# An earlier rank for the work that feeds TensorE, in a four-layer attention kernel on one core

## The chip, the core and the metric

The kernel runs on one core of a Trainium2 chip. A core has TensorE (matrix products, written to PSUM), VectorE, ScalarE, GpSimd and the DMA queues, the busiest of which is issued by SyncE (SP). The profile calls them PE (with PEld for weight loads), DVE, ACT, POOL and SP. The metric is the device time of one execution in microseconds: lower is better. All data are 32-bit floats.

## The reference

The input x has 16 samples of 256 channels by 32 x 32 positions (1024 tokens). Four layers follow each other.

```python
# layer 0: group norm, self-attention over 1024 tokens of width 256, projection, residual
xn = group_norm(x, gamma, beta)
q, k, v = jnp.split(jnp.einsum('bchw,oc->bohw', xn, w_qkv) + b_qkv[None, :, None, None], 3, axis=1)
attn = jax.nn.softmax(jnp.einsum('bnc,bcm->bnm', q, k) / math.sqrt(C), axis=-1)
out = jnp.einsum('bnm,bmc->bnc', attn, v)
x = jnp.einsum('bchw,oc->bohw', out, w_proj) + b_proj[None, :, None, None] + residual
# layer 1: a gate of one value per position
weight3 = jax.nn.relu(_conv3x3(jnp.concatenate([mean_c(x), max_c(x)], axis=1), w1, b1))
x = x * jax.nn.sigmoid(_conv3x3(mean_c(x) + max_c(x) + weight3, w2, b2))
# layer 2: as layer 0 with its own weights
# layer 3: q and k of width 32, logits clipped to [-10, 10], softmax, v of width 256
energy = jnp.clip(jnp.einsum('bqn,bqm->bnm', q, k) * scale, -10.0, 10.0)
x = gamma[0] * jnp.einsum('bcm,bnm->bcn', v, jax.nn.softmax(energy, axis=-1)) + x
```

Here `mean_c` and `max_c` stand for the mean and the maximum over channels.

## The kernel before

**Tiling.** Tokens are tiled in 8 tiles of 128, channels in 2 chunks of 128. Query-key weights and value-projection weights are multiplied together once at the start (`fold`, `fold3`), so that an attention has one product for t, one for the logits, one for the values and one for the weighted sum. The larger products are made with seven block products in place of eight. This needs combinations of blocks: sums and differences of the left blocks (`combine`, L902 to L905), of t (`logits`, L642 to L645), of the values (`value_sums`, L557 to L561) and of the exponentials (`weighted`, L698, L699, L746, L751), made by VectorE. A block of the result is the sum of several products in different PSUM banks. In `seven`, ScalarE copies one bank out (`copy`; L672 in the logits, L925 in the values, L947 for t) and VectorE adds the other bank to it (`plus`, L603). `weighted` has the same with L743, L756, L759 and L768 as copies, L725 as sums, and the reciprocals of the row sums at L755 and L762. All matrix products of these helpers are recorded on one line, L571. The eight PSUM banks are one pool.

**The stages of one sample** (`sample`): load; norm of layer 0 (`group_norm`, called by `head`); attention of layer 0 (`attend`: t, values, then for each half of the queries `logits` with exponentials L682 and L684, and `weighted`, which adds the normalised result to the residual at L732); planes for the gate (L992, L1000); the gate (`gate_of`) and its scaling (L1018, L1022); a turn from token order to channel order by VectorE transposes (L519) and a DMA through memory on the SP queue (`send`); norm of layer 2; attention of layer 2; another turn and send; layer 3 (`clipped_attend`: q and k at L1072 with their bias at L1084 and L1088, values, logits at L1107 with exponentials L1123 and clip L1128, `weighted`); strip transposes (L494), bias (L487) and the store. `attend` and `weighted` serve layers 0 and 2; `weighted` serves layer 3, too.

**The order of the work.** The program text is written as Python generators. Two lanes, one for even and one for odd samples, take turns: each `yield` hands over to the other lane, and lane 1 starts 30 steps (`OFFSET`) behind lane 0. Constants W_* put empty steps into a lane at places with a long latency, such as the gate and the sends; `chores` are small pieces of work handed out one a step. The order in which instructions are written gives each its rank. The framework's planner then goes through the program with its own estimates of durations: whenever an engine comes free, it issues, of the instructions for that engine whose inputs are ready, the one of the lowest rank. What comes out is a fixed order for each engine, and each engine keeps to it on the chip, waiting on semaphores for its inputs. `keep_in_program_order` holds an instruction behind all that is written before it on its engine.

An alternative path for inputs outside of the fast path's range (`general_path`) is in the program, but doesn't run here.

## Time and profile before

| what | value |
|---|---|
| time, median of 3 runs | 2700.45 us (2700.41 to 2702.32) |
| span of the profiled execution | 2702.3 us |
| the profiled execution's own time | 2702.32 us, the slowest of the three |
| instructions | 47717 |
| mean granted TensorE clock | 0.997 of full |
| bytes read from memory, written | 69.58 MB, 50.33 MB |
| matmuls, VectorE and ScalarE instructions | 18998, 4242, 2810 |

The page of the profile gives each engine's busy time and its share of the span; a table by stretches gives the same within a stretch, with the number of instructions in brackets, then the granted clock, the busy share of the DMA engines and GB/s. A line of waits reads "who waited <- for whom: us in total, times, longest us". A line in order of time reads "start, us, engine, line, operation, what it writes <- what it reads, partitions x elements, count", and in square brackets the idle time of the engine before it and what ended it.

### The profile page before, as it was taken

The page shows a single profiled execution, that of the slowest core. Times are in us where ns is not written, and L with a number is a line of the kernel's source. Part 1 is how long each engine was busy: PE and PEld are TensorE (multiplying, and loading weights), DVE is VectorE, ACT ScalarE, POOL GpSimd, SP SyncE. Part 2 cuts the span into 40 slices and gives each one's busy share as a digit, 9 for nine tenths or more (in the row PEclk, how much of TensorE's full clock was granted, in tenths as well). Part 3 has the DMA queues.
Part 4 walks back from the last instruction along what each step waited for, and adds up shares of the span by engine and source line. Part 5 has one row for each costly group of instructions (what it writes and reads, how often), then busy time and mean ns, then how long its engine had stood idle before and what let it go on. Part 6 is the DMA issues. An engine that isn't in the chain of part 4 may idle for free.

```text
span 2702.3 us, 47717 instructions
## 1 busy us (share of the span) xinstructions
PE 2658.2 (98%) x18998; PEld 2366.0 (88%) x18998; DVE 2153.9 (80%) x4242; ACT 1327.9 (49%) x2810; POOL 45.4 (2%) x118
## 2 busy tenths in 40 slices
PE   8999999999999999999999999999999999999997
PEld 6888988888988889889889898988989889898897
DVE  7988886888778887788867888678887788868776
ACT  3454455544455445544455544554454544545443
POOL 1000000000000000000000000000000000000000
PEclk9999999999999999999999999999999999999999
DMA  4021111212111120211201212112111121101111
GB/s 115 1 63 48 56 32 24 63 48 63 25 46 50 42 76 9 55 48 48 63 16 48 63 35 61 32 32 63 48 48 32 32 63 55 40 17 34 52 34 41
DMA packets 134823, 123.07 MB, mean 46 GB/s; under 512 B 10689, under 2 KB 125633, under 8 KB 134593
## 3 DMA queue, kind: packets, MB, share of 16 engines
q1 hardware_dynamic: 132720, 118.63, 15.7%
q8 instruction: 152, 2.49, 0.4%
q10 hardware_dynamic: 1872, 1.31, 0.2%
q14 instruction: 79, 0.64, 0.1%
HBM read 69.58 MB, written 50.33 MB: 44 GB/s over the span
## 4 chain that ended last, share of the span: by engine, by line
PE 81%; DVE 13%; ACT 4%; issue 2%; DMA 1%; POOL 0%; DVEq 0%; SPq 0%; ACTq 0%
PE b_l L571 15%; PE c_l L571 11%; PE af_l L571 11%; PE sb_l L571 10%; PE sc_l L571 8%; PE sf_l L571 4%; PE sa_l L571 3%; PE vb_l L571 3%; PE tb_l L571 3%; PE vc_l L571 2%; PE tc_l L571 2%; PE s L1107 2%; DVE e_l L603 1%; DVE vt L603 1%; PE vf_l L571 1%
## 5 line engine op out<-in xcount | busy, mean ns | idle before, releaser
L672 ACT COPY e_l<-sb_l 128x512 f32<-128x512 f32 x384 | 222.5, 584 | 217.9 <-PE sb_l L571 216.7
L571 PE MATMUL sb_l<-t_l,x 128*128 128x256 f32 x1024 | 262.0, 386 | 0.3
L571 PE MATMUL b_l<-vt,e_l 128*128 128x128 f32 x2048 | 251.8, 275 | 0.0
L571 PEld LDWEIGHTS b_l<-vt,e_l 128*128 128x128 f32 x2048 | 244.2, 192 | 5.4 <-issue 2.3
L571 PEld LDWEIGHTS sb_l<-t_l,x 128*128 128x128 f32 x1024 | 180.5, 191 | 40.1 <-ACT e_l L672 11.2
L682 ACT ACTIVATE e_l<-e_l 128x512 f32<-128x512 f32 x256 | 160.9, 630 | 86.6 <-DVE e_l L603 85.7
L684 ACT ACTIVATE e_l<-e_l 128x1024 f32<-128x1024 f32 x128 | 135.5, 1059 | 118.4 <-DVE e_l L603 118.4
L571 PE MATMUL c_l<-tv,cb_l 128*128 128x129 f32 x1536 | 189.0, 275 | 0.2 <-DVE cb_l L698 0.2
L571 PEld LDWEIGHTS c_l<-tv,cb_l 128*128 128x128 f32 x1536 | 180.3, 191 | 6.9 <-PE qk L1072 3.1
L603 DVE TENSOR_TENSOR e_l<-sc_l,e_l 128x512 f32<-128x512 f32 x128 | 88.0, 687 | 116.6 <-PE sc_l L571 114.9
L925 ACT COPY vt<-vb_l 128x512 f32<-128x512 f32 x144 | 84.5, 587 | 147.2 <-PE vb_l L571 146.1
L487 ACT ACTIVATE xr<-xr,bstrip 128x128 f32<-128x128 f32 (+1 forms) x376 | 134.4, 443 | 44.1 <-DVE xr L494 44.1
L1123 ACT ACTIVATE e<-s 128x512 f32<-128x512 f32 x256 | 131.8, 606 | 22.1 <-PE s L1107 21.4
L756 ACT COPY acc_l<-c_l 128x256 f32<-128x256 f32 x96 | 35.4, 368 | 212.3 <-DVE ri_l L755 151.8
L571 PE MATMUL sc_l<-tc_l,xs_l 128*128 128x256 f32 x512 | 134.0, 384 | 2.3 <-DVE vt L603 2.3
L571 PE MATMUL af_l<-tv,e_l 128*128 128x128 f32 x1024 | 131.6, 278 | 4.3 <-ACT e_l L682 4.3
L571 PE MATMUL sc_l<-t_l,xs_l 128*128 128x256 f32 x512 | 133.0, 382 | 0.8
L571 PE MATMUL sa_l<-t_l,x 128*128 128x256 f32 x512 | 132.4, 381 | 0.0
L571 PE MATMUL sf_l<-tc_l,x 128*128 128x256 f32 x512 | 131.7, 380 | 0.0
L571 PE MATMUL sb_l<-tc_l,xs_l 128*128 128x256 f32 x512 | 131.7, 379 | 0.0
L571 PEld LDWEIGHTS af_l<-tv,e_l 128*128 128x128 f32 x1024 | 121.3, 192 | 10.8 <-ACT e_l L682 7.7
L1128 DVE TENSOR_SCALAR e<-e 128x1024 f32<-128x1024 f32 x128 | 83.0, 687 | 59.0 <-ACT e L1123 59.0
(245 smaller groups left out, 5984.6 us busy)
## 6 DMA issues: line engine op xcount, KB each, us to landing
x<-mid_x SPq DMA_DIRECT2D x64, 512.0 KB, 3.3
xr<-in_x_dram SPq DMA_DIRECT2D x64, 256.0 KB, 4.9
mid_x<-t_z SPq DMA_DIRECT2D x128, 128.0 KB, 2.3
mid_x<-t_l SPq DMA_DIRECT2D x128, 128.0 KB, 2.3
x<-in_x_dram SPq DMA_DIRECT2D x62, 256.0 KB, 4.0
out_dram<-xr SPq DMA_DIRECT2D x124, 128.0 KB, 2.3
raw_l<-in_w_l_dram SPq DMA_DIRECT2D x1, 1024.0 KB, 6.9
raw_l<-in_w_l_dram SPq DMA_DIRECT2D x2, 256.0 KB, 5.5
```

Of the source, the lines that this page charges most:

```text
L487: nc.scalar.activation(y[:, s, ts], y[:, s, ts], AF.Identity, bias=bias[:, s : s + 1])
L571: mm = nc.tensor.matmul(out, left, right, start=fresh and m == 0 and (lone or i == 0), stop=(m == len(pairs) - 1), skip_group_check=True,)
L603: nc.vector.tensor_tensor(dst, src, dst, ALU.add)
L672: nc.scalar.copy(block(i, j), ps.rearrange("p (m n) -> p m n", m=2))
L682: nc.scalar.activation(part, part, AF.Exp)
L684: nc.scalar.activation(e[:, m : m + 2, :], e[:, m : m + 2, :], AF.Exp)
L756: nc.scalar.copy(acc[:, hi, c2], c[:, :, :P])
L925: nc.scalar.copy(block(i, j), ps.rearrange("p (m n) -> p m n", m=TPH))
L1107: nc.tensor.matmul(ss[g][:, j * 2 * P : (j + 1) * 2 * P].rearrange("p (t g j) -> p t g j", t=TPH, g=2), qk[gs, mh, 1 - blk, j * P : (j + 1 ...
L1123: nc.scalar.activation(by_strip[:, :, :, qa], ss[g].rearrange("p (m t n) -> p m t n", m=2, t=TPH), AF.Exp,)
L1128: nc.vector.tensor_scalar(part, part, EXP_MIN, EXP_MAX, ALU.max, ALU.min)
```

## The change

A block `with soon():` is put around instructions of VectorE, ScalarE and (one in each norm) GpSimd. Inside such a block an instruction gets a rank that is 100 lower than its place in the program text; after the block the rank goes on where it was before it. Matrix products, DMAs and everything outside of the blocks keep their rank. The planner is otherwise the same, and so are the instructions and their dependencies.

In the blocks are: all of `group_norm` (the general path passes `ExitStack`, which does nothing), `value_sums`, the sums of `seven`, the combinations, copies and exponentials of `logits`, the combinations, copies, sums and reciprocals of `weighted`, `combine`, and the copies of `values` and of t. Not in them are: the additions L732, planes, gate and scaling, turns, strip transposes and bias, the weight folding, the checks, and of layer 3 the q and k writes (L1084, L1088), the exponentials (L1123) and the clip (L1128).

```diff
+URGENT = 100
...
+    soon = functools.partial(tc.high_priority, offset=URGENT)
...
-def group_norm(nc, k, small, xt, out, gamma, beta, nm, keep=None):
+def group_norm(nc, k, small, xt, out, gamma, beta, nm, soon, keep=None):
...
+    with soon():
+        st = small.tile([P, CC, 2, 6], FP, tag="st", name=f"st_{nm}", bufs=2)
...
     yield
...
+    with soon():
+        rst = small.tile([P, 6], FP, tag="rst", name=f"rst_{nm}", bufs=2)
...
     yield
...
+    with soon():
+        a = small.tile([P, CC], FP, tag="a", name=f"a_{nm}")
...
             t1, t2, t4 = (tv[:, i, :, :P] for i in range(3))
-            nc.vector.tensor_tensor(t1, b[0][1], b[0][0], ALU.subtract)
...
+            with soon():
+                nc.vector.tensor_tensor(t1, b[0][1], b[0][0], ALU.subtract)
...
-                nc.vector.tensor_tensor(dst, src, dst, ALU.add)
+                with soon():
+                    nc.vector.tensor_tensor(dst, src, dst, ALU.add)
...
+            with soon():
+                nc.vector.tensor_tensor(t1, t3, bl(0, 0), ALU.subtract)
...
-                    nc.scalar.copy(block(i, j), ps.rearrange("p (m n) -> p m n", m=2))
+                    with soon():
+                        nc.scalar.copy(block(i, j), ps.rearrange("p (m n) -> p m n", m=2))
...
                     if step >= 2:
+                        with soon():
+                            m = (step - 2) * TPH + 2 * g
...
+            with soon():
+                nc.vector.tensor_tensor(s1, a(1, 0), a(1, 1), ALU.add)
+                nc.vector.tensor_tensor(s3, a(0, 0), s3, ALU.subtract)
...
             def plus(ts, cs, ps):
-                nc.vector.tensor_tensor(acc[:, ts, cs], ps, acc[:, ts, cs], ALU.add)
+                with soon():
+                    nc.vector.tensor_tensor(acc[:, ts, cs], ps, acc[:, ts, cs], ALU.add)
...
             c = bank(f"c_{nm}_{h}")[:, : 2 * (P + 1)].rearrange("p (i c) -> p i c", i=2)
             go(s1, t1, c, lone=False)
+            with soon():
+                nc.vector.reciprocal(ri[:, n1 : n1 + 2], c[:, :, P])
+                nc.scalar.copy(acc[:, hi, c2], c[:, :, :P])
             yield
...
+            with soon():
+                nc.vector.tensor_tensor(left("s1"), left("21"), left("22"), ALU.add)
...
             def copy(i, j, ps):
-                nc.scalar.copy(block(i, j), ps.rearrange("p (m n) -> p m n", m=TPH))
+                with soon():
+                    nc.scalar.copy(block(i, j), ps.rearrange("p (m n) -> p m n", m=TPH))
...
             def t_copy(i, j, ps):
+                with soon():
+                    nc.scalar.activation(
+                        t_block(i, j),
```

## The prediction

> **What bounds the kernel now.** I read the first part of the page (busy shares), then the same in three stretches, then TensorE's waits, then the order of time at the places where TensorE stood still. Busy shares and stretches:
>
> ```profile
> span 2702.3 us, 47717 instructions
> PE 2658.2 (98%) x18998; PEld 2366.0 (88%) x18998; DVE 2153.9 (80%) x4242; ACT 1327.9 (49%) x2810; POOL 45.4 (2%) x118
> ...
> 0.00:100.00 100.00, 86.36 (x466) 71.03 (x467) 81.03 (x244) 42.02 (x81) 12.01 (x38) 0.97 0.31 78
> 100.00:2600.00 2500.00, 2485.08 (x17790) 2214.18 (x17788) 2004.31 (x3880) 1248.69 (x2643) 32.75 (x77) 1.00 0.16 45
> 2600.00:2702.00 102.00, 86.73 (x747) 80.74 (x745) 68.57 (x120) 37.20 (x87) 0.60 (x3) 0.96 0.12 33
> ```
>
> In each stretch the first figure after its length is TensorE's busy time. TensorE is the bound: idle 13.6 us in the first 100, 15.3 us in the last 102 and only 14.9 us in the 2500 between. That understates its stalls, because a matmul's record is longer than its place in the stream: 16 matmuls of 128 columns fill 1.95 us with records of 275 ns each, so they start every (1950 - 275) / 15 = 112 ns, and a stall of up to 275 - 112 = 163 ns shows no idle time. I therefore took the starts themselves from the trace. Between 100 and 2600 us, starts that came more than 60 ns later than the usual spacing after their predecessor's shape (the 32-row logits of layer 3 left out) add up to 75.4 us. Sorted by the semaphore that came last and by what its engine did before: 29.1 us follow no semaphore, 9.2 us follow TensorE itself, 18.1 us follow a ranked instruction (one that the change moves) whose engine had been idle, 8.3 us a ranked one queued behind another ranked one, 8.0 us a ranked one queued behind an unranked one, and 2.7 us an unranked one. Only the 8.0 us are directly what the change addresses.
>
> TensorE's waits over the whole run:
>
> ```profile
> PE fold_l L322 <- DVE wt_l L316: 7.4, 3, 6.8
> PE wtp_l L311 <- DMA raw_l<-in_w_l_dram: 4.5, 1, 4.5
> PE af_l L571 <- ACT e_l L682: 4.3, 16, 0.3
> PE b_l L571 <- DVE e L1128: 4.2, 3, 1.9
> ...
> PE vc_l L571 <- DVE xs_l L902: 2.3, 1, 2.3
> PE sc_l L571 <- DVE vt L603: 2.3, 7, 0.3
> ```
>
> The columns are total us, times, longest. The first two are the start-up, where weights are loaded and folded; neither line is ranked. The waits on L682, L902 and L603 follow ranked lines. The wait on L1128, the clip of layer 3, follows a line that is not ranked.
>
> The one long wait at a ranked line, in the order of time, VectorE and TensorE:
>
> ```profile
> 2645.28 1.25 DVE L494 STREAM_TRANSPOSE xr<-xr 128x1024 f32<-128x1024 f32 x1
> ...
> 2646.56 1.49 DVE L1088 TENSOR_SCALAR t_qk<-qk,qb 64x256 f32<-64x256 f32 x3
> ...
> 2648.08 0.69 DVE L603 TENSOR_TENSOR vt<-va_l,vt 128x512 f32<-128x512 f32 x1
> 2648.69 0.68 DVE L902 TENSOR_TENSOR xs_l<-x 128x512 f32<-128x512 f32 x1
> ...
> 2649.42 1.53 PE L571 MATMUL vc_l<-vc_l,xs_l 128*128 128x128 f32 x8 [2.28 <-DVE xs_l L902]
> ```
>
> TensorE stands 2.28 us for the first combination (L902), which VectorE starts only after a strip transpose (L494) and three bias adds (L1088), both unranked.
>
> **What the change moves.** Nothing is added or removed; no instruction changes length. Counted by line, 2944 of VectorE's 4242 instructions (1775 of 2409 us of summed records) and 1633 of ScalarE's 2810 (980 of 1487 us) get the earlier rank, and 32 powers on GpSimd. What remains behind is about a quarter of VectorE's work and a third of ScalarE's: the normalised additions L732 (184 us), turns L519 and L494 (88 and 78), planes L992 and L1000 (39 and 77), bias adds L487 (166), the gate, and four lines that do feed TensorE in layer 3: the clip L1128 (88), its exponentials L1123 (155), and the q/k writes L1088 and L1084 (47 and 45). With three quarters of VectorE ranked alike, the order among ranked instructions stays what it was.
>
> Term 1, ranked behind unranked, 100 to 2600 us: 8.0 us at most, 0 at least, below nothing not from this term (its loss is term 5). An instruction already running isn't interrupted, and the unranked ones ahead take 0.44 (L487) to 1.25 us (L494), so a quarter may stay: I take -6.0.
>
> Term 2, the 18.1 us at ranked instructions whose engine was idle: there the delay lies a step upstream (the exponential L682 waits for the sum L603). Of the queued ranked ones 8.0 of 16.3 us were behind unranked ones, 0.49; I give half of the chains to a queue at all and half to TensorE itself: 18.1 x 0.49 x 0.5 = -4.4. Ends 0 and -18.1.
>
> Term 3, the end. The combination need not stand behind L494 and L1088: up to 2.3 us. After that stall the granted clock was 0.83 over 2650 to 2660 us, which is 10 x 0.17 = 1.7 us of TensorE. Ends 0 and -4.0; I take -3.0, nearer to the full price, as the blocking instructions are plainly unranked. The Trainium skill, TensorE: Matmul & The Clock Gate, section "Why this matters for your kernels", says that the clock is lost by idle gaps over some 3 us; by that, 2.28 us would cost no clock and the term would be 2.3 at most, while here the clock fell after it, so the trace disagrees.
>
> Term 4, the start. The 11.9 us of fold and weight DMA stay. Between 50 and 60 us TensorE is busy 8.60 and the clock granted is 0.66, 1.4 and 3.4 us. There the unranked fold and its bias (L417 to L437) compete with sample 0's ranked sums: earlier sums may fill the gap (-4.8), later folding may widen it by as much (+4.8). I take 0.
>
> Term 5, the four unranked lines of layer 3 now yield to the other lane's ranked work. Floor 0. Ceiling: one 0.69 us sum (L603) ahead of the clip in each of 16 samples x 2 halves x 2 key halves is 64 x 0.69 = 44 us, if the other lane gave TensorE nothing meanwhile. It does: at an offset of 30 steps the other lane is in an attention of layer 0 or 2 then, and the present waits at unranked lines are 2.7 us. I take them doubled, +2.7. At the very end no other lane covers, but the clip's 4.2 us of waiting there lies behind exponentials and older sums, whose order stays.
>
> Moved past without cost: on GpSimd, 2% busy, only the power L138 (0.70 us each) passes counting instructions. No DMA is ranked, but the sends on SP wait for the turn L519, which yields: their x<-mid_x transfers start later by about one 0.7 us sum each, hidden by the other lane as long as TensorE has its products. Ranked norms pass older additions L732; their readers, planes and gate, have 9 steps of planned distance.
>
> Sum: -6.0 - 4.4 - 3.0 + 0 + 2.7 = -10.7 on the profiled 2702.3 us, which is the slowest of the three runs and has nothing around it (2702.32 against a span of 2702.3): 2691.6. It lies 1.9 us above the median, so against the median run I predict 2690 us. Ends of all terms: -35 and +49.
>
> **Rivals.** A difference under 0.2% (5.4 us) can hardly be told from none here.
>
> A, forecast: the small gain, 2690 us, alone between 2676 and 2695.
>
> B, exchange: every stall removed is replaced by another, because a product starts the moment its producer is done. For it: in the trace a third of TensorE's semaphore waits ended less than 0.2 us before the matmul began, so the new order will have its own near misses. Against: 8.0 us have an unranked instruction plainly in the way. 2700 us.
>
> C, layer 3 starves (slower): clip, exponentials and q/k writes fall so far behind that TensorE runs out of the other lane's products too. For it: the clip is already the longest wait outside the start-up fold (1.9 us); VectorE is at 80%, so what yields waits long. Against: TensorE's 99.4% in the middle. It decides when more than (10.7 + 2.7) / 0.69, about 20, of the 64 key halves are uncovered; at half, 32 x 0.69 = 22 us in place of 2.7: 2700.4 - 13.4 + 22 = 2709, and with the gain of terms 1 to 3 absent 2722.
>
> D, blocked queue (slower): ranked instructions are set early where their input is late, and all behind them stand. VectorE shows it now:
>
> ```profile
> DVE ri L762 <- PE c_l L571: 67.7, 25, 4.5
> DVE ri_l L762 <- PE c_l L571: 65.3, 25, 4.6
> ```
>
> Fifty times, 2.7 us each, VectorE idles at a reciprocal for TensorE. If ten such waits more stood before a sum that TensorE needs, 27 us less the gain of 10.7: 2717. Against: VectorE has 548 us idle in all. The same page of the Trainium skill, section "Architectural detail: the array is 16× 32×32, not 1× 128×128", calls the two engines' queues strictly first in, first out; that speaks against ranking by estimates: were all 50 waits doubled it would charge VectorE 133 us, 85% of the span, still not the bound.
>
> **How the numbers follow.** A 0.47, B 0.18, C 0.25, D 0.10: faster by over 0.2% 0.47, same 0.18, slower 0.35. The range 2674 to 2716 takes A to just under its low end (terms 1 and 3 in full and 14.5 of term 2's 18.1: 2700.4 - 8 - 4 - 14.5 = 2674), B, and C to between its two cases; it leaves D's 2717 and C's upper end out, some 0.17.
>
> **What would show it.** Right: TensorE's idle between 100 and 2600 us falls from 14.9 to about 10 us, waits at L682 and L603 shrink; near the end L902 runs ahead of L494 and L1088, and the clock there stays at 1.00. L1128 and L1088 start later after their exponentials and products. Wrong: TensorE's waits at L1128, L1123 or L1084 grow beyond 13 us together (C), VectorE's idle at TensorE grows while TensorE waits at sums (D), or the start loses more than 5 us.

## The result and the profile after

| | before | changed |
|---|---|---|
| time, median of 5 runs each on one chip | 2701.08 us (2700.41 to 2702.94) | 2725.76 us (2720.43 to 2726.35) |
| ratio | 1 | 1.0079, interval 1.0067 to 1.0090 |
| span of the profiled execution | 2702.3 us | 2718.6 us |
| TensorE idle, 0 to 100 / 100 to 2600 / rest | 13.6 / 14.9 / 15.3 us | 18.3 / 26.8 / 12.9 us |

The change made the kernel 0.8% slower; the forecast was 2690 us. The profiled execution is the fastest of the changed kernel's five (2720.43 us, 1.8 above its span), so the profiles show 16.3 us of the 24.7 between the medians.

Line numbers have moved. In the changed kernel the products of all helpers are L577 (L571 before), the sums of `seven` L610 (L603), the weighted sums L737 (L725), the additions that end `weighted` L744 (L732), scalings on VectorE L1044 (L1022), turns L524 (L519), the first statistics of a norm L116 (L114), its last VectorE step L149 (L145), the weight copies of the fold L321 (L316), score copies L681 (L672) and exponentials L692 (L682). The experiments' kernels differ from it by a few lines more.

The first lines of the page after, and the table by stretches:

```profile
span 2718.6 us, 47720 instructions
PE 2660.1 (98%) x18998; PEld 2365.2 (87%) x18998; DVE 2160.5 (79%) x4242; ACT 1330.4 (49%) x2810; POOL 42.5 (2%) x118
...
0.00:100.00 100.00, 81.74 (x452) 67.16 (x453) 80.00 (x242) 40.99 (x78) 10.73 (x38) 0.97 0.31 78
100.00:2600.00 2500.00, 2473.24 (x17676) 2201.19 (x17676) 1999.30 (x3859) 1242.97 (x2629) 31.14 (x77) 1.00 0.16 44
2600.00:2718.00 118.00, 105.10 (x874) 96.84 (x873) 81.16 (x143) 46.40 (x104) 0.60 (x3) 0.95 0.14 37
```

The work is the same: TensorE's busy time differs by 1.9 us, the middle's clock not at all. What has grown is time in which TensorE stands. TensorE's waits after:

```profile
PE fold_l L327 <- DVE wt_l L321: 7.1, 3, 6.0
PE fold_l L327 <- DVE ve_l L137: 6.6, 1, 6.6
PE tb_l L577 <- PE sb_l L577: 6.3, 8, 0.8
PE tb_l L577 <- ACT t_l L969: 4.8, 8, 0.6
...
PE af_l L577 <- ACT e_l L692: 3.8, 15, 0.3
PE sc_l L577 <- DVE vt L610: 3.8, 7, 0.5
PE b_l L577 <- DVE e L1150: 3.6, 3, 1.6
PE sb_l L577 <- ACT e_l L681: 3.0, 8, 0.4
...
PE vc_l L577 <- DVE xs_l L922: 1.6, 1, 1.6
```

The entries with a count of 8 are the steady state: 16 samples run in two lanes, so the same thing happens eight times, once per pair of samples. I took the start of the gate's first product (c_l<-rows) of every second sample as a mark and split the span with it:

| stretch | before | changed | difference |
|---|---|---|---|
| start to the first gate product | 132.5 us | 135.4 us | +2.95 |
| seven periods of a pair of samples | 2309.1 (329.9 to 330.2 but for the first, 329.3) | 2321.2 (331.5 to 331.9) | +12.1 |
| from the last such mark to the last instruction | 260.8 | 262.0 | +1.2 |

The differences add up to 16.3, the whole difference of the spans. So there are two questions: what costs 1.7 us in every period (12.1 over seven), and what costs time at the start.

**The period.** In each pair, the second lane's t product of layer 2 (tb_l) comes late. Counted from the gate product of its period it starts at 84.57 us before and at 86.66 after. Before it stands the norm of layer 2, before that the send, the turn, the scaling, and the gate. Here are VectorE's instructions in order of time, first of the kernel before (its period starts at 791.78 us):

```profile
850.05 1.30 DVE L519 STREAM_TRANSPOSE t_z<-xr 128x512 f32<-128x512 f32 x2
...
866.80 0.17 DVE L762 RECIPROCAL ri_l<-c_l 128x2 f32<-128x2 f32 x1 [2.76 <-PE c_l L571]
866.89 0.40 DVE L725 TENSOR_TENSOR acc_l<-c_l,acc_l 128x256 f32<-128x256 f32 x1
867.33 0.88 DVE L732 SCALAR_TENSOR_TENSOR xr<-acc_l,ri_l,xr 128x256 f32<-128x256 f32 x2
868.13 1.28 DVE L114 BATCH_NORM_STATS2 st_l<-x 128x6 f32<-128x512 f32 x2
...
869.43 0.37 DVE L725 TENSOR_TENSOR acc_l<-b_l,acc_l 128x256 f32<-128x256 f32 x1
...
869.83 0.37 DVE L725 TENSOR_TENSOR acc_l<-af_l,acc_l 128x256 f32<-128x256 f32 x1
...
870.24 0.65 DVE L603 TENSOR_TENSOR e_l<-sa_l,e_l 128x512 f32<-128x512 f32 x1
...
873.34 0.69 DVE L603 TENSOR_TENSOR e_l<-sc_l,e_l 128x512 f32<-128x512 f32 x1
...
874.83 0.69 DVE L603 TENSOR_TENSOR e_l<-sb_l,e_l 128x512 f32<-128x512 f32 x1
875.44 0.80 DVE L145 TENSOR_SCALAR x<-x,a_l,bb_l 128x1024 f32<-128x1024 f32 x1
```

and then of the changed kernel (its period starts at 798.80 us):

```profile
857.09 0.65 DVE L610 TENSOR_TENSOR e_l<-sb_l,e_l 128x512 f32<-128x512 f32 x1
857.67 0.67 DVE L610 TENSOR_TENSOR e_l<-sf_l,e_l 128x512 f32<-128x512 f32 x1
858.31 0.69 DVE L610 TENSOR_TENSOR e_l<-sa_l,e_l 128x512 f32<-128x512 f32 x1
858.91 0.34 DVE L1044 TENSOR_SCALAR xr<-xr,sg_l 128x256 f32<-128x256 f32 x1
859.29 1.30 DVE L524 STREAM_TRANSPOSE t_z<-xr 128x512 f32<-128x512 f32 x2
...
873.63 0.17 DVE L780 RECIPROCAL ri_l<-c_l 128x2 f32<-128x2 f32 x1 [2.29 <-PE c_l L577]
873.72 0.41 DVE L737 TENSOR_TENSOR acc_l<-c_l,acc_l 128x256 f32<-128x256 f32 x1
...
875.75 0.42 DVE L737 TENSOR_TENSOR acc_l<-b_l,acc_l 128x256 f32<-128x256 f32 x1 [0.71 <-ACT acc_l L787]
876.09 0.41 DVE L737 TENSOR_TENSOR acc_l<-af_l,acc_l 128x256 f32<-128x256 f32 x1
876.42 1.27 DVE L116 BATCH_NORM_STATS2 st_l<-x 128x6 f32<-128x512 f32 x2
...
877.73 0.63 DVE L610 TENSOR_TENSOR e_l<-sa_l,e_l 128x512 f32<-128x512 f32 x1
...
880.71 0.68 DVE L610 TENSOR_TENSOR e_l<-sc_l,e_l 128x512 f32<-128x512 f32 x1
...
882.62 0.68 DVE L610 TENSOR_TENSOR e_l<-sb_l,e_l 128x512 f32<-128x512 f32 x1
...
883.29 0.68 DVE L610 TENSOR_TENSOR e_l<-sf_l,e_l 128x512 f32<-128x512 f32 x1
...
883.96 0.68 DVE L610 TENSOR_TENSOR e_l<-sa_l,e_l 128x512 f32<-128x512 f32 x1
884.56 0.80 DVE L149 TENSOR_SCALAR x<-x,a_l,bb_l 128x1024 f32<-128x1024 f32 x1
```

Two displacements are seen. First, the last scaling and turn, which have no rank, run behind three sums of scores that have one: the turn starts 60.5 us into the period in place of 58.3, and the data of the send behind it land at 71.0 in place of 69.35. Second, the statistics of this data start at 77.6 in place of 76.35, and not because the data are late: they have been there for 6.6 us (7.0 us in the kernel before). In both kernels the statistics stand in VectorE's fixed order behind the weighted sum of c_l, for whose product VectorE idles (2.76 us before, 2.29 us here). In the changed kernel two more weighted sums stand ahead of them, those of b_l and af_l, with another 0.71 us of waiting for ScalarE; and between the statistics and the norm's last step there are five score sums where there were three. Together that is 2.1 us, and TensorE starts tb_l 0.1 us after this last step in both kernels:

```profile
883.54 1.13 PE L577 MATMUL sb_l<-tc_l,xs_l 128*128 128x256 f32 x4 [0.38 <-ACT e_l L681]
885.46 1.10 PE L577 MATMUL tb_l<-x,m_l 128*128 128x512 f32 x2 [0.79 <-PE sb_l L577]
```

The page names TensorE's own sb_l as the releaser, but the product reads the norm's output, written until 885.36.

Not all of the 2.1 us is lost. In the kernel before, the four matmuls of sb_l that end ahead of tb_l here run behind it (at 881.58 us); at 216 ns from start to start they are 0.9 us of work done earlier. Taking each matmul's start against the usual spacing after its predecessor's shape, as the prediction did, TensorE loses 1.2 us more than before up to tb_l, and 0.5 us more in the rest of the period, at smaller waits such as that at sc_l behind a value sum (0.5 us, 0.3 before). These two make up the 1.7 us.

**The start.** A product of the fold waits 6.02 us (0.34 us in the kernel before) for copies of its weights (L321), which VectorE takes behind ranked work of sample 0 and a strip transpose. The other long wait in the list, 6.6 us at the fold's first product, isn't new: it is 6.8 us in the kernel before, where the page names L316 as the releaser. VectorE's order behind the wait of 6.02 us:

```profile
39.06 0.69 DVE L610 TENSOR_TENSOR vt<-vb_l,vt 128x512 f32<-128x512 f32 x1 [0.44 <-ACT vt L946]
...
41.47 0.68 DVE L565 TENSOR_TENSOR tv<-vt,tv 128x512 f32<-128x512 f32 x1
42.07 2.36 DVE L499 STREAM_TRANSPOSE xr<-xr 128x1024 f32<-128x1024 f32 x2
44.35 0.12 DVE L356 TENSOR_SCALAR tb_l<-tbp_l 128x2 f32<-128x2 f32 x1
44.40 0.74 DVE L321 COPY wt_l<-wtp_l 128x256 f32<-128x256 f32 x2
```

### The profile page after: what moved, and what is told of

Same layout as the page of the kernel before. It is cut to its first block, busy times and chain, and to the rows that moved or that the text cites. A ratio compares the mean times of both kernels' runs of the same rounds, so it can differ in the third digit from the quotient of the medians.

```text
span 2718.6 us, 47720 instructions
## 1 busy us (share of the span) xinstructions
PE 2660.1 (98%) x18998; PEld 2365.2 (87%) x18998; DVE 2160.5 (79%) x4242; ACT 1330.4 (49%) x2810; POOL 42.5 (2%) x118
## 4 chain that ended last, share of the span: by engine, by line
PE 83%; DVE 11%; ACT 4%; issue 1%; DMA 0%; POOL 0%; DVEq 0%; SPq 0%
PE b_l L577 17%; PE sb_l L577 12%; PE c_l L577 12%; PE af_l L577 11%; PE sc_l L577 8%; PE sf_l L577 4%; PE sa_l L577 4%; PE vb_l L577 3%; PE tb_l L577 2%; PE vc_l L577 2%; PE s L1129 2%; DVE vt L610 1%; PE tc_l L577 1%; PE qk L1094 1%; PE va_l L577 1%
## 5 line engine op out<-in xcount | busy, mean ns | idle before, releaser
L681 ACT COPY e_l<-sb_l 128x512 f32<-128x512 f32 x384 | 222.1, 584 | 209.7 <-PE sb_l L577 207.4
L577 PE MATMUL sb_l<-t_l,x 128*128 128x256 f32 x1024 | 261.3, 387 | 0.4
L577 PE MATMUL b_l<-vt,e_l 128*128 128x128 f32 x2048 | 251.4, 275 | 0.5 <-ACT acc_l L776 0.5
L577 PEld LDWEIGHTS b_l<-vt,e_l 128*128 128x128 f32 x2048 | 243.5, 192 | 5.8 <-issue 2.3
L577 PEld LDWEIGHTS sb_l<-t_l,x 128*128 128x128 f32 x1024 | 180.8, 191 | 43.4 <-ACT e_l L681 13.8
L692 ACT ACTIVATE e_l<-e_l 128x512 f32<-128x512 f32 x256 | 160.2, 629 | 98.6 <-DVE e_l L610 97.9
L694 ACT ACTIVATE e_l<-e_l 128x1024 f32<-128x1024 f32 x128 | 135.4, 1058 | 118.6 <-DVE e_l L610 117.8
L577 PE MATMUL c_l<-tv,cb_l 128*128 128x129 f32 x1536 | 188.9, 275 | 0.0
L577 PEld LDWEIGHTS c_l<-tv,cb_l 128*128 128x128 f32 x1536 | 180.3, 191 | 6.5 <-PE qk L1094 3.1
L610 DVE TENSOR_TENSOR e_l<-sc_l,e_l 128x512 f32<-128x512 f32 x128 | 87.5, 684 | 105.7 <-PE sc_l L577 103.1
L577 PE MATMUL sc_l<-tc_l,xs_l 128*128 128x256 f32 x512 | 133.1, 382 | 3.8 <-DVE vt L610 3.8
L577 PE MATMUL sb_l<-tc_l,xs_l 128*128 128x256 f32 x512 | 132.4, 381 | 3.0 <-ACT e_l L681 3.0
L577 PE MATMUL af_l<-tv,e_l 128*128 128x128 f32 x1024 | 130.9, 278 | 3.8 <-ACT e_l L692 3.8
L577 PE MATMUL sc_l<-t_l,xs_l 128*128 128x256 f32 x512 | 133.2, 382 | 0.2 <-ACT e_l L681 0.2
L577 PE MATMUL sa_l<-t_l,x 128*128 128x256 f32 x512 | 131.5, 379 | 0.0
L577 PE MATMUL sf_l<-tc_l,x 128*128 128x256 f32 x512 | 131.4, 379 | 0.0
L577 PE MATMUL b_l<-vt,e 128*128 128x128 f32 x1024 | 127.6, 278 | 3.6 <-DVE e L1150 3.6
L577 PEld LDWEIGHTS af_l<-tv,e_l 128*128 128x128 f32 x1024 | 121.3, 192 | 9.7 <-ACT e_l L692 6.3
```

Source lines behind the costliest of these rows:

```text
L577: mm = nc.tensor.matmul(out, left, right, start=fresh and m == 0 and (lone or i == 0), stop=(m == len(pairs) - 1), skip_group_check=True,)
L610: nc.vector.tensor_tensor(dst, src, dst, ALU.add)
L681: nc.scalar.copy(block(i, j), ps.rearrange("p (m n) -> p m n", m=2))
L692: nc.scalar.activation(part, part, AF.Exp)
L694: nc.scalar.activation(e[:, m : m + 2, :], e[:, m : m + 2, :], AF.Exp)
```

## The experiments

The theory to be tested, called G in what follows: ranked VectorE work pushes back the unranked chain of gate, scaling, turn and send, the norm and the t product behind it come late, and TensorE has nothing else to do. Against it stood these: that a stall taken away in one place comes up in another whatever one does (E), that other unranked or ranked instructions are the cause (layer 3's feeders, the prediction's rival C; the exponentials, X; the additions that end `weighted`, J; the fold's copies; the norm, N), and that the loss comes from how the start sets the lanes against each other (S). Each run's time is a ratio to the kernel before on the same chip, with its 95% interval; "first gate" is the start of the first gate product, "periods" the seven periods together (2309.1 us before, 2321.2 changed).

### e1 to e4: one more kind of instruction ranked, or one fewer

e1 ranks the copies and scaled products of the fold, too:

```diff
-                    nc.vector.tensor_copy(wt[:, j, o, :], ps[:, :C])
+                    with soon():
+                        nc.vector.tensor_copy(wt[:, j, o, :], ps[:, :C])
...
-                    nc.vector.tensor_scalar(dst[:, c, :], ps[:, :C], scale, None, ALU.mult)
+                    with soon():
+                        nc.vector.tensor_scalar(dst[:, c, :], ps[:, :C], scale, None, ALU.mult)
```

> The changed kernel, with the copies and scalings of the weight folding (fold: the copies of the transposed weights and the scaled products) ranked too. Theory S (the loss at the start, some 3 to 5 us, is unranked folding behind ranked sums): the 6.0 us wait of TensorE at the third fold copy, at 38.8 us, goes; the first sample's gate products come 3 to 4 us earlier (132 in place of 135.4 us); the period of a pair of samples stays at 331.6 us; total 3 to 4 us below the changed kernel. Rival R (any new order just scatters the near misses): the start changes by an arbitrary amount, up or down by 3 us, and the period also.

Measured: 2720.23 us, ratio 1.0058 (1.0041 to 1.0075). The 6.0 us wait for the copies is gone, yet the first gate product comes at 135.2, as in the changed kernel; TensorE now stands at other places of the start (1.4 us at a bias, for instance, 0.7 before). Periods 2320.9: the steady state does not care.

e2 takes the rank from the exponentials of `logits`:

```diff
                     if step >= 2:
-                        with soon():
+                        with ExitStack():
```

> The changed kernel with the exponentials of the logits back at their own place in the text. Theory X (in each pair of samples the 1.06 us exponential now runs on ScalarE ahead of the copy that frees TensorE's PSUM bank): the 0.54 us stall before the product of t-combinations goes and the stall after it before t's first product falls from 0.95 to about 0.6 us, so the period falls from 331.6 to about 330.7 us and the total by 6 to 8 us; TensorE's waits on the copy L681 go from 3.0 us to under 1. Rival R: the period moves by an arbitrary amount with other stalls in its place; no fall of more than 2 us expected.

Measured: 2722.87 us, 1.0072 (1.0055 to 1.0089), periods 2320.8. The waits at score copies stay (3.0 us, 8 times). The exponentials' rank isn't the cause.

e3 ranks the additions that end `weighted`:

```diff
             def done(i):
...
-                nc.vector.scalar_tensor_tensor(
+                with soon():
+                    nc.vector.scalar_tensor_tensor(
```

> The changed kernel with the normalised additions (the scalar_tensor_tensor in done, unranked so far) ranked too. Theory J (the additions yield to ranked work on VectorE, the plane sums on ScalarE wait for them, and the ranked copy of t stands behind the plane sums in ScalarE's fixed order): the stall of 0.77 us before t's last product, eight times, goes; TensorE's wait on the copy of t falls from 4.8 us to under 1; the period falls from 331.6 to about 330.8 us, the total by about 6 us. Rival R: no such fall, the stall stays or others of its size come.

Measured: 2723.73 us, 1.0076 (1.0060 to 1.0093), periods 2320.3. The 4.8 us at the copies of t, which stood on ScalarE behind plane sums that waited for these additions, are gone, and TensorE stands elsewhere in their place. A local cause, rightly named, and no gain.

e4 ranks layer 3's feeders: q and k writes, exponentials, clip:

```diff
+                with soon():
                     for to, src, blk in ((low, low, 0), (g2, g0, 0), (g2, g1, 1)):
...
+                    with soon():
                         for a in range(2):
                             m = mh * TPH + 2 * a
```

> The changed kernel with the q and k writes, exponentials and clip of layer 3 ranked too. The prediction's rival C (layer 3's unranked feeders starve): the total falls by 10 us or more, towards the kernel before or under it. Theories S, X and J: layer 3 holds only 0.2 and 0.3 us of the new stalls of a period (the sum behind the clip, the copy behind an exponential), so the total falls by at most 4 us and can rise, as more ranked work queues behind ranked work; the start stays as it is.

Measured: 2722.73 us, 1.0068 (1.0051 to 1.0085), periods 2320.7. Rival C of the prediction is refuted as the cause: these four lines yield no more when they are ranked, and nothing comes back.

### e5: the gate's end, the scalings and the turns ranked

```diff
                for t in range(h * TPH, (h + 1) * TPH):
-                    if t % 2:
+                    with soon():
+                        if t % 2:
...
-                turn(xr, z[:, h], h)
+                with soon():
+                    turn(xr, z[:, h], h)
                 send(z, x1, slice(h, h + 1), f"x1_{b}_{h}")
```

(and in `gate_of`, for this call, the exponentials, the addition and the reciprocal at its end)

> The changed kernel with three more kinds of instruction ranked: the exponentials, addition and reciprocal that end the gate, the eight scalings of xr, and the turns behind them in each sample (not the gate's products, not the DMAs). Theory G (the ranked VectorE work pushes the unranked chain of gate, scaling, turn and send back; the norm and the t product behind it start later, and TensorE has nothing else to do): the last scaling of the second lane comes back from 60.1 us to 57.5 or less after the first gate product of its period, that norm ends at 84 or less instead of 85.8, the period of a pair of samples falls from 331.5 to 330.0 or less, and the time to 2705-2713. Rival E (a stall that is taken away in one place comes up in the next, since the orders of three engines no longer fit each other): the chain is earlier but the period stays at 331.2-331.8, the time at 2716-2726. Rival D (these ranked instructions stand in the queue ahead of sums that TensorE waits for): above 2726.

Measured: 2708.55 us, 1.0022 (1.0011 to 1.0032), periods 2309.6. Three quarters of the loss is gone, and in the steady state all of it in sum: by the starts, TensorE loses 0.4 us less than in the kernel before up to tb_l, and still 0.2 to 0.4 us more behind it. VectorE's order around the second lane's norm (period from 796.51 us):

```profile
855.03 1.30 DVE L525 STREAM_TRANSPOSE t_z<-xr 128x512 f32<-128x512 f32 x2
...
868.93 1.26 DVE L116 BATCH_NORM_STATS2 st_l<-x 128x6 f32<-128x512 f32 x2
...
871.97 0.37 DVE L738 TENSOR_TENSOR acc_l<-c_l,acc_l 128x256 f32<-128x256 f32 x1
...
879.01 0.77 DVE L149 TENSOR_SCALAR x<-x,a_l,bb_l 128x1024 f32<-128x1024 f32 x1
```

The turn is at 58.5 again, all statistics now stand ahead of the weighted sums, the norm's last step ends 83.3 us into the period (86.6 in the changed kernel), and tb_l follows at 84.2 without a wait. Of TensorE's waits with a count of 8, the one at tb_l behind sb_l and the one at the score copies are both gone. What remains is the start: first gate product at 136.8, and 14.2 us of waits of the fold's products (7.4 in the kernel before, 13.7 in the changed one).

### e6: the norms unranked

```diff
-                nc, k, small, by_chunk, by_chunk, L0_GAMMA, L0_GAMMA + 1, f"l0_{b}", soon, keep
+                nc, k, small, by_chunk, by_chunk, L0_GAMMA, L0_GAMMA + 1, f"l0_{b}", ExitStack, keep
```

(and the same for layer 2)

> The changed kernel with the norms of both layers at their places again; all other ranks stay. Theory G: the norm is only the last part of a chain that is late already; unranked it is later still, so the period is 331.5 or more and the time 2720-2732. Rival N (the 20 or so ranked VectorE instructions of each norm are what pushes sums and turns back): the period falls to 330.5 or less and the time to 2703-2713. Rival E: the period stays at 331.2-331.8, the time at 2716-2726.

Measured: 2726.04 us, 1.0082 (1.0065 to 1.0099), periods 2323.6. The norms' rank doesn't cause the loss; without it the periods are 0.3 us longer each. First gate product at 139.3.

### e7: ranks only from the third sample on

```diff
-    soon = functools.partial(tc.high_priority, offset=URGENT)
+    on = []
+
+    def soon():
+        return tc.high_priority(offset=URGENT) if on else ExitStack()
...
+            if b >= 2:
+                on.append(b)
             xt, xr = ready.pop(b)
```

> The changed kernel with the ranks given only from the third sample on: the two first samples' first layers and all of the fold are written as in the kernel before. The loss in the profiles is 2.9 us up to the first gate product, 2.2 in the first period, and 1.6 in each of the seven or so after it. If start and steady state are two separate losses (theory G and rival E both say so): first gate product at 132.5, periods of 331.3-331.7 from the second or third pair on, time 2713-2719. If the loss of the steady state comes from the way the two lanes are set against each other at the start (rival S): periods of 330.0-330.4 throughout, time 2700-2706.

Measured: 2716.39 us, 1.0047 (1.0030 to 1.0064), first gate product at 130.7, the first period 329.3, all others 331.5 to 331.8. Start and steady state are two separate losses; S is refuted. By subtraction from the changed kernel's 1.0079 the start is worth some 0.3% of the time, 8 to 9 us (either ratio is known to between 0.1 and 0.2%), more than the 2.95 us between the two profiles.

### e8: nothing but the chain ranked

This is the kernel before with the ranks of e5 for the gate's end, scalings, turns, and the change's ranks for the norms, and no others.

> The kernel before with only the chain ranked: the end of the gate, the scalings, the turns behind them and the norms; no sums, copies, combinations or exponentials. Theory G: the norm of the second lane ends 1-2 us earlier than in the kernel before (83.7 after the first gate product), where 0.6 us of waits stood at the t product behind it; the period falls to 329.3-330.0, the time to 2693-2701. Rival E: some other wait takes it, 330.1-331.0 and 2701-2709. If it is above 2709, ranking this chain costs the sums more than it gives.

Measured: 2705.03 us, 1.0013 (1.0003 to 1.0022), periods 2310.0. The norm's last VectorE step ended at 80.8 us into the period in place of 84.5, but tb_l started at 84.8: earlier than TensorE can take it, the norm is worth nothing. In the kernel before, the chain ended just at the edge, so it could lose by being pushed; pulled ahead, it had only the 0.44 us that TensorE idles at tb_l to gain, and TensorE's waits at exponentials rose from 4.3 to 6.8 us instead.

### e9, e10: e5 with ranks from the third sample on, and with the additions

e9 joins the edits of e5 and e7; e10 adds that of e3.

> The kernel of e5 (gate end, scalings and turns ranked with the rest), with all ranks given only from the third sample on. Theory G with a separate loss at the start: first gate product at 130-133, periods 329.7-330.1, last gate to end 254-255, time 2698-2704, which is the kernel before again. If ranks in the steady state gain anything beyond undoing their own damage: periods below 329.5 and below 2696. If start and steady state are not separate: first gate at 136 or periods above 330.5, 2706-2716.

Measured: 2700.83 us, 0.9993 (0.9984 to 1.0002), periods 2309.8. Both losses mended, the time is that of the kernel before. (Its profiled execution had the first gate product at 135.2, with a granted clock of 0.76 and 0.90 between 50 and 70 us; at 2705.17 us it was the slowest of eleven.)

> The kernel of e9 with the scaled additions that end each weighted product ranked too. In the kernel of e5 the t product still waits 4.8 us (8 times) for a ranked copy on ScalarE that stands behind plane sums, which wait for these additions; ranked alone they gave nothing, when the turns were late. Theory G: with the turns in time this wait is the next limit, and 0.3-0.6 us go from each period (329.4-329.7), 2694-2701. Rival E: the wait goes and another takes its place, period 329.8-330.2, 2698-2704.

Measured: 2701.15 us, 0.9988 (0.9979 to 0.9998), periods 2308.6. The wait at the copies of t goes, as in e3, and now 0.16 us of each period go with it: rival E's figure rather than G's.

### e11, e13: a delay put into the chain of the kernel before

```diff
-                turn(xr, z[:, h], h)
+                for _ in range(4 if lane and h else 1):
+                    turn(xr, z[:, h], h)
                 send(z, x1,
```

(e13; e11 has the turn twice. The repeats write the same result.)

> The kernel before, with no ranks, in which the second half of the turn behind the gate is done twice in the second lane only (two VectorE instructions of about 0.7 us more in the chain, once in a period; the result is the same). It puts a delay of about 1.4 us into the chain and changes nothing else. Theory G (this chain has no slack at the second lane's t product, so its delay is TensorE's): the norm of that lane ends 1.0-1.4 us later and the period grows by 0.7-1.4, to 330.7-331.4; time 2705-2712. Rival E (it is the changed order of sums and copies that costs; the chain has slack): period 329.8-330.3, time 2699-2704.

Measured: 2703.35 us, 1.0000 (0.9990 to 1.0009), periods 2307.8. The data land 0.8 us later, the statistics start 0.5 later, the norm ends on time.

> The kernel before, no ranks, with the second half of the turn behind the gate done four times in the second lane (six VectorE instructions of 0.6-0.7 us more, about 3.7 us of delay in the chain once in a period; the result is the same). In the changed kernel the last turn there is 2.2 us late, and with the turn done twice (1.2 us) the norm still ended on time. Theory G (lateness of this chain beyond some 1.2 us is TensorE's): norm end 2 us later or more, period 331.0-332.5, time 2708-2720. Rival Q (real lateness is absorbed, what costs is only the order in VectorE's queue that the ranks give): period 329.6-330.2, 2699-2705.

Measured: 2712.59 us, 1.0027 (1.0017 to 1.0037), periods 2314.9, 0.8 us each. But the norm isn't what is late. The data land at 72.4 us, 3.1 later than in the kernel before and 1.4 later than in the changed kernel; the statistics start at 76.6 (76.35 before) and the norm ends on time (84.6). What TensorE waits for is another thing:

```profile
PE af_l L571 <- ACT e_l L684: 13.6, 8, 1.7
```

The exponentials of the other lane are late by the time that the repeated turns took VectorE from the sums in front of them. So e13 can't give the price of a late turn by itself; what it does show is that late data alone, later than in the changed kernel, did not make the norm late. Theory G as I had put it, lateness handed down the chain, falls. What the changed kernel's norm waits for is its place in VectorE's order.

### e12: ranks of 30 in place of 100

```diff
-URGENT = 100
+URGENT = 30
```

> The changed kernel with ranks of 30 instructions in place of 100. Theory G: fewer ranked VectorE instructions pass the scalings and turns, so the chain is pushed back by less: the last scaling of the second lane at 57.4-60.1 after the first gate product, period 330.0-331.3, time 2703-2718. If the size of the rank does not matter (any rank inverts the order): 331.4-331.7, 2718-2726.

Measured: 2714.30 us, 1.0044 (1.0029 to 1.0060), first gate product at 130.9, periods 2319.8. At this size the start's loss is gone: the fold's copies stand ahead of sample 0's value sums again, and the product that waited 6.02 us waits 0.30. The steady state is as bad as with 100, its chain the same within 0.2 us. My expectation that the push shrinks with the rank was wrong there.

### e14: the norms ranked by 300

```diff
+    sooner = functools.partial(tc.high_priority, offset=300)
...
-                nc, k, small, by_chunk, by_chunk, L2_GAMMA, L2_GAMMA + 1, f"l2_{b}", soon
+                nc, k, small, by_chunk, by_chunk, L2_GAMMA, L2_GAMMA + 1, f"l2_{b}", sooner
```

(so for layer 0, too)

> The changed kernel with the norms ranked 300 instructions ahead in place of 100, all else equal. In the changed kernel the second half's statistics in the second lane stand in VectorE's queue behind three sums that wait for TensorE, though their data landed 6.6 us earlier, and five sums of the scores stand among the norm's last steps. If the norm's rank against these sums puts them there (rival N): statistics before the sums, period 330.0-330.5, 2703-2712. If the scheduler places the norm by when it expects the data, which the late turns set (theory G): the place of the second lane's norm and the period of 331.3-331.7 stay, 2716-2726.

Measured: 2733.22 us, 1.0109 (1.0092 to 1.0126), periods 2334.2. The second lane's norm stands at the very same place, statistics at 77.63 and last step at 85.76 us, so even a rank of 300 against the sums' 100 doesn't get it ahead of them; rival N is refuted. That the scheduler holds it back because it expects the data late, I only argue. The further 1.9 us a period go elsewhere, above all into TensorE's waits behind ScalarE's copies in `weighted` (8.2 us, 19 times, 2.4 in the changed kernel); I did not follow them up.

### e15: ranks of 30, with e5 and e3, in all samples

> The changed kernel with ranks of 30, and the gate's end, the scalings, the turns behind them and the scaled additions ranked as well. The rank of 30 gave a first gate product at 130.9 (135-141 in the runs with 100 from the first sample on), the ranked turns a period of 329.9. If both losses are separate and mended so: first gate product 130-132, periods 329.5-330.2, time 2697-2704. If they are not separate: 2706-2716.

Measured: 2700.32 us, 0.9992 (0.9982 to 1.0001), first gate product at 129.8, periods 2307.4, 0.2 us each below the kernel before. With the chain of gate, scaling, turn and norm ranked like the sums, and ranks of 30, the change costs nothing and gains nothing that can be told from none.

### e16: the sums of `seven` unranked, all other ranks kept

```diff
-                with soon():
-                    nc.vector.tensor_tensor(dst, src, dst, ALU.add)
+                nc.vector.tensor_tensor(dst, src, dst, ALU.add)
```

> The changed kernel with one rank taken away: the sums of seven products (into scores, values and t) stand at their places again; weighted sums, copies, combinations, exponentials and norms stay ranked. In the changed kernel four of these sums stand ahead of the second lane's last scaling and turn, five among its norm. Theory G with these sums as what passes the turns: the last scaling at 57.5-58.5 after the first gate product, period 329.9-330.5, time 2705-2713 (the start's loss stays). If other ranked work pushes the turns: period 331.2-331.7, 2718-2726.

Measured: 2712.38 us, 1.0024 (1.0012 to 1.0035), first gate product at 137.8, periods 2312.9. Taking away this one rank gives back 8.3 of the 12.1 us: last scaling at 57.6, turn 58.4, statistics at 76.5 ahead of the two weighted sums, the norm's last step from 83.8, all within 0.2 us of the kernel before. The periods are 330.1 to 330.6, so some 0.5 us each comes from other ranks; by the starts, 0.1 to 0.2 us of it is lost up to tb_l and 0.3 to 0.6 us behind it. TensorE's wait at tb_l is there by its right name, and small:

```profile
PE tb_l L577 <- DVE x L149: 3.2, 8, 0.4
```

### What the runs add up to

| ranks | first gate, us | seven periods, us | ratio |
|---|---|---|---|
| none (before) | 132.5 | 2309.1 | 1 |
| the change | 135.4 | 2321.2 | 1.0079 |
| less the sums of `seven` (e16) | 137.8 | 2312.9 | 1.0024 |
| 30 (e12) | 130.9 | 2319.8 | 1.0044 |
| from the third sample (e7) | 130.7 | 2319.2 | 1.0047 |
| with turns (e5) | 136.8 | 2309.6 | 1.0022 |
| with turns, from the third sample (e9) | 135.2 | 2309.8 | 0.9993 |
| 30, with turns and additions (e15) | 129.8 | 2307.4 | 0.9992 |

Shown: the steady loss comes of ranked work against an unranked end of the gate, unranked scalings and turns (e5 takes all of it away), and two thirds of it need the ranked sums of `seven` (e16); it doesn't depend on the size of the rank (30 or 100), the norms' rank, the exponentials, layer 3 or the start. The start's loss needs a rank of 100 on the work of the first samples: in all nine profiles that have it on sums or copies, the first gate product comes at 135.2 to 140.9 us, in eight of the nine without (e8, which ranks only the chain, among them) at 129.8 to 132.5; the ninth is e9. The means of the nine are 137.8 and 131.1, 6.7 us apart; the medians of the times say 1.0079 less 1.0047 or 1.0044, and 1.0022 less 0.9993 (e5 and e9), 8 to 10 us. Executions of one kernel differ by as much (2700.9 to 2709.1 us in 22 of the kernel before), so this price is rough. Left open: why the scheduler puts the second half's statistics behind the weighted sums once the turns are late, when e13's even later data do not lead there; which of the three that e5 ranks (the gate's end, the scalings, the turns) it needs; and which of the ranks costs at the start once the fold's copies are ranked (e1).

## Why the prediction was wrong

**Direction.** It gave 0.47 to a gain and 0.35 to a loss, and its range of 2674 to 2716 lies under the 2725.8 measured. Two steps failed.

The first is "Moved past without cost". It saw that the sends wait for the turn L519, which yields, priced this at about one 0.7 us sum, and called it hidden by the other lane. The turn came 2.2 us later, behind three sums and not one. And the other lane hid only 0.9 of the 2.1 us by which tb_l came late; for the other 1.2 us TensorE stood. tb_l was already the product at which TensorE waited for a norm, with 0.44 us idle ahead of it in the kernel before:

```profile
876.35 1.10 PE L571 MATMUL tb_l<-x,m_l 128*128 128x512 f32 x2 [0.44 <-PE sa_l L571]
```

That line could be had beforehand. It names sa_l as the releaser, and I took it for TensorE's own; what the product reads, and that VectorE's L145 ends 0.1 us before it, would have shown a chain without slack.

The second is "the order among ranked instructions stays what it was", so that no term priced a change of it. The statistics, the weighted sums and the score sums are all ranked, and their order changed: two more weighted sums stand ahead of the statistics, and two more score sums between these and the norm's last step. This order is what made the norm late, not its data (e13). e5 and e16 show that the missing rank of the chain and the rank of the sums bring it about; by what step of the planner is open. The term that was missing is 1.7 us a period, 12.1 us over seven.

**Term 1** (ranked behind unranked, -6.0 of 8.0 us). The class didn't shrink, it grew, from 8.0 to 13.8 us, by the same tally of late starts; ranked behind ranked went from 8.3 to 16.2. Named stalls of the kernel before did go, for instance one of 0.3 us at scores (sc_l) in the third period, and e3 shows a wait taken away clean. But in each case others came. Rival B, exchange, describes this; it left out that the exchange can be a bad one.

**Term 2** (-4.4 of 18.1 us). 14.7 after, -3.4: about the size, and worth nothing in a sum whose other members grew. All late starts between 100 and 2600 us went from 75.4 to 91.2 us.

**Term 3** (the end, -3.0). The combination did not pass: VectorE still ran one bias add, the strip transpose and a value sum ahead of it, only two of the three bias adds moved behind. The wait went from 2.28 to 1.65 us, 0.6 us in place of 3.0. The clock stayed at 1.00 up to 2670 us, behind this stop, and was 0.83 over 2670 to 2680 us, where TensorE stopped once more, for 1.3 us, so this trace shows no gain of clock. "The blocking instructions are plainly unranked" was true and not enough: a rank decides only among the instructions whose inputs the planner holds ready at that moment. That this is why the combination did not pass, I only argue.

**Term 4** (the start, 0 between -4.8 and +4.8). The ends were right in kind: the fold yielded to sample 0's sums, 6.0 us at one product. The profile says +2.95, the means of nine profiles 6.7, the medians some 8 to 10. The upper end of 4.8 was the size of a gap that was there already, and nothing held the loss to it: the one wait alone grew by 5.7 us, from 0.34 to 6.02, and the 11.9 us of fold and weight DMA that were to stay became 18.3. The prediction's mark, more than 5 us lost at the start, was the right one to watch.

**Term 5 and rival C** (layer 3's feeders, +2.7, or 22 and more). TensorE's wait at the clip is 3.6 us, 4.2 before, and e4 changes nothing. The unranked feeders that starved TensorE were not those of layer 3 but those of layer 2: in the chain of gate, scaling, turn, send and norm only the last had been counted as feeding TensorE.

**Rival D** (blocked queue, 2717). Its picture, instructions in place while their input is late and others standing behind, is the one nearest to what happened: the statistics behind weighted sums, the first of which waits for TensorE. It was given 0.10 and had been worked out for sums that TensorE needs, not for the norm. The 50 waits at the reciprocals, its own mark, did not grow (67.8 and 60.6 us after).

**The clock and the queue.** In the changed kernel's end the granted clock was 0.83 over 2670 to 2680 us. The longest stop in the 20 us before was that of 1.65 us, which ends at 2665.9 us; the nearest one is 1.3 us long and ends at 2675.4. So this trace, too, disagrees with the 3 us or so that the Trainium skill, TensorE: Matmul & The Clock Gate, section "Why this matters for your kernels", gives as the gap that costs clock. Nor do these traces give a shorter gap as the rule: in the kernel before, stops of 1.9 us (ending at 2661.0) and 1.6 us (at 2678.0) left the clock at 1.00 from 2660 to 2690 us. And VectorE kept to its order where that was costly: statistics whose data had landed 6.6 us earlier stood behind a reciprocal that waited 2.29 us for TensorE, and the sums behind it. This agrees with the strict first-in, first-out queues of VectorE and ScalarE in the same page's section "Architectural detail: the array is 16× 32×32, not 1× 128×128", which the prediction had cited against the change and then judged harmless by VectorE's idle time.

## What to carry to other kernels

A rank given to some of an engine's work is a delay for the rest, so before ranking what an engine waits for, follow each of the unranked instructions to its last reader. In this kernel a chain that ends in the bounding engine (gate, scaling, turn, norm) cost 12.1 us over seven periods while its first links were left out, and nothing when it was ranked as a whole (e5) or not at all. Nor does the order among ranked instructions stay as it was when others move around them. Look for the place with no slack first: a product that starts within 0.1 us of its producer's end is one, whatever releaser the page names. And when the bounding engine idles for 0.6% of the steady state, and its late starts add up to 3% (75.4 of 2500 us), an order can gain no more than that, while the loss has no such limit: even the best of these orders (e10, 0.9988) is within what can hardly be told from none.

## What was not expected of the hardware

Nothing in the engines themselves; what surprised was how much the start of the same program can differ: seven of the profiles (the kernel before, e7 to e11 and e13) have the same order of TensorE, VectorE and ScalarE up to the first gate product, and it came between 129.9 us (e11) and 135.2 us (e9). Between e10 (130.0 us) and e9 the granted clock differs: 0.83 and 0.76 between 50 and 60 us, 1.00 and 0.90 between 60 and 70. And real lateness was absorbed more easily than a changed order: 3.1 us of later data (e13) left the norm's end where it was, while the changed kernel, with data 1.7 us later, had it 2.1 us later. (The repeated turns of e13 cost TensorE 0.8 us a period at another place.)
